# A decoder's state-space branch: its preparation cut into steps, and the second layer's moved beside the first attention

## The chip, the core and the metric

The kernel runs on one core of a Trainium2 chip. The core has five engines that each run their own instructions in order: TensorE (PE in the profile, with its weight loads as PEld), VectorE (DVE), ScalarE (ACT), GpSimd (POOL) and SyncE (SP, which issues most transfers). They wait for each other by semaphores. The metric is the time of one execution in microseconds (us), median of several runs.

## The reference

A decoder of four layers works on x, 4 batches of 256 tokens by 256 features, in float32. Each layer has an attention or a recurrence, a second branch that looks at a context, and a feed-forward part; each adds to x, and x is normalised after it. The change touches the first two layers:

```python
x = LN(x + attn0(x))            # multi-query attention, 16 heads of 128, rotary
x = LN(x + ssm0(context, z=x))  # selective state-space scan of the context
x = LN(x + thought(x))          # 4 iterations on the last token, gated into all tokens
x = LN(x + attn1(x))            # grouped-query attention (GQA), 16 heads of 16, 4 key heads
x = LN(x + ssm1(context, z=x))  # the same kind of scan with other weights
x = LN(x + moe(x))
```

The state-space branch takes only the context, until its last line, where x comes in as a gate:

```python
u     = silu(conv4(in_proj(context)) + conv_b)        # 256 channels e
dt, Bm, Cm = split(x_proj(u))                         # 8, 16 and 16 rows
delta = softplus(dt_proj(dt) + dt_proj_b)
A     = -exp(A_log)                                   # [256, 16]
state = state * exp(delta * A) + (delta * u) * Bm     # over the 256 tokens, 16 states n
y     = sum_n(state * Cm) + D * u
out   = y * silu(x)
```

So everything up to y can be worked out at any time before the gate, and only the gate and the sum into x stand in the layer's order.

## The kernel before

**Attention of layer 0, `run_mqa` (from L232).** 32 turns n, eight to a batch, each for four heads and one half of the batch's queries. A turn scales the shares of its softmax (reciprocal `sm`, L320), makes the scores of turn n + 1 and the queries of turn n + 4 (L281, from a PSUM pool `pm` of one bank), takes two scan steps (`K.scans.beside(2)`), turns the shares, projects turn n - 1 (`output`) and sums over the values (`sums`, copied out at L342). Turns 2 to 5 also make values and keys that are still missing.

**The scans, class `Scans` (L398 to 531).** The branch of a layer has a preparation and 64 scan steps (4 batches by 16 states). The preparation: four products of the convolution's taps with the input projection (four loads, four multiplications on GpSimd); the convolution as matrix products, in four groups of 128 channels by 512 tokens, each with an activation out of PSUM; Silu over the whole `u`; x_proj (copied at L474, stored to DRAM at L476 to be spread over the partitions later); dt_proj with a sum into `delta` (L115) and the absolute value into `du`; Exp, Ln and a maximum (L120) that make softplus; and `du = delta * u` on GpSimd. All of it is issued at once by `begin`. One scan step: a transfer of Bm and Cm rows to all partitions (`bc`, L513), two Exp on ScalarE (`dA`), a product on GpSimd (`s`, by the helper `ptt`, L123), the scan itself on VectorE (L520), a product with Cm (`s`, helper `tt`, L111), and, two steps later, a matrix product with the identity that adds it up in one PSUM bank (`ssmps`, helper `mm`, L132). `bc` and `s` have four buffers each, `dA` three. At the 16th state of a batch D * u is added (`u<-u,..,ssmps`, L120).

**The gate, `gate_pair` (L534).** It first takes scan steps until batch b is complete (`upto`), then Silu(x), a product on GpSimd, four transposes and the sum into x with its normalisation (`add_out`, `settle`, POOL's `rstd`). In the whole program the gates of layer 0 stand inside `run_mqa`, at turn 2 of the second batch after theirs began, the last behind turn 31; then the preparation of layer 1 is issued. Those of layer 1 stand inside the GQA.

**The thought, `run_thought` (L585).** First the gate (8 tiles: matrix products, additions of `gate_b`, one Sigmoid, L674 to 680), then the last token (`tok`, L686) and its normalisation, then four iterations of small operations that depend on each other (`tT` begins each, on [128, 8] tiles), and `lastmean`. GpSimd works out `gx` and `xb` from the gate and x, 24 scan steps are issued, and the result is gated into all tokens and normalised.

**GQA, `run_gqa` (L982).** A front part of eight tiles (products, rotary products `t0` to `t3`), each with a scan step, then 32 steps of the heads (`SmallHeads.run`), each with a scan step; a reciprocal `rec` (L915) ends each of eight units of four steps.

The order on each engine is made by a planner from the order of issue: an operation that is issued earlier has precedence, but a later one may go first where the planner expects it to be ready. So the place where the code takes a scan step is not exactly the place where the step stands on the engines.

## Time and profile before

| what | value |
|---|---|
| median of 3 runs | 2512.23 us (2508.54 to 2512.66) |
| profiled execution | 2505.99 us, span 2504.2 us |
| MQA, last reciprocal L320 | 380.9 us |
| layer 0's scans | 88.6 to 381.6 us |
| layer 1's scans | 467.4 to 771.4 us |
| thought, `tok` to `lastmean` | 431.8 to 519.6 us |
| GQA, first rotary product to end | 572.6 to about 800 us |

The page gives each engine's busy time and its share of the span. An engine that is busy for a large share isn't the bound everywhere: a stage can be bound by TensorE, and the next by a chain of small operations. A group's row gives line, engine, operation, output and inputs, how often, the duration of one (least, median, greatest in ns) and its first and last start. The program's later stages, from 800 us on, hold none of the edited code; they are two thirds of the span.

### The profile page before, as it was taken

Reading aid. Unit: us, or ns where it says so; the run is one execution under the profiler, and the core shown is the slowest. Engines: PE = TensorE matmul, PEld = TensorE weight load, DVE = VectorE, ACT = ScalarE, POOL = GpSimd, SP = SyncE. Lnnn points to the kernel's source line nnn. Section 1 sums busy time; section 2 is a strip of 40 time slices with the busy share of each in tenths; the row PEclk is TensorE's granted clock in tenths of the full one; section 3 lists DMA queues with packets and bytes.
Section 4 is the critical chain, followed back from the end, with each engine's and each line's share of the span. In section 5 each row is a group of like instructions: output and inputs, shape, how many; then the busy total and the mean of one; then the engine's idle time right before and its main releaser. Section 6 shows DMA issues by size and latency. Waiting matters only on the chain. (4 is left out here: it accounts for less than half of the span.)

```text
span 2504.2 us, 28859 instructions
## 1 busy us (share of the span) xinstructions
PE 2277.2 (91%) x10624; PEld 1526.3 (61%) x10624; DVE 1460.8 (58%) x2824; ACT 802.4 (32%) x1781; POOL 530.6 (21%) x617
## 2 busy tenths in 40 slices
PE   8798988648996999989999999999999989799997
PEld 5466654224443565545888888888776544476774
DVE  3798984588875412182356454444555667774556
ACT  3566663422442111153111111111122244343434
POOL 2544543663332222210001100011110002100001
PEclk9899999677987999999999999999988899999999
DMA  5221221122223254230123111211100002100000
GB/s 197 60 60 45 57 54 40 41 61 42 52 46 109 88 158 130 66 112 29 45 66 110 48 58 45 71 46 47 46 22 1 20 18 70 40 1 1 1 1 17
DMA packets 132836, 138.99 MB, mean 56 GB/s; under 512 B 13876, under 2 KB 120726, under 8 KB 130904
## 3 DMA queue, kind: packets, MB, share of 16 engines
q1 hardware_dynamic: 132696, 137.16, 19.1%
q8 instruction: 84, 1.38, 0.2%
q14 instruction: 56, 0.46, 0.1%
HBM read 134.27 MB, written 2.85 MB: 55 GB/s over the span
## 5 line engine op out<-in xcount | busy, mean ns | idle before, releaser
L132 PE MATMUL ps<-xw,xcT 128*128 128x256 f32 (+1 forms) x2304 | 519.0, 382 | 0.3 <-ACT YT L126 0.3
L132 PEld LDWEIGHTS ps<-xw,xcT 128*128 128x128 f32 x2304 | 430.7, 190 | 64.2 <-issue 1.9
L132 PE MATMUL sc<-kT,qT 32*128 32x256 f32 (+2 forms) x1024 | 240.7, 412 | 11.1 <-DVE qn L129 10.7
L520 DVE TENSOR_TENSOR_SCAN s<-dA,s 128x512 f32<-128x512 f32 x128 | 210.3, 1666 | 35.6 <-POOL s L123 35.4
L123 POOL TENSOR_TENSOR s<-du,bc 128x512 f32<-128x512 f32 x128 | 178.9, 1410 | 231.0 <-PE ssmps L132 191.1
L132 PEld LDWEIGHTS sc<-kT,qT 128*128 128x128 f32 (+1 forms) x1024 | 152.9, 206 | 92.3 <-issue 57.8
L132 PE MATMUL ssmps<-s,idz 128*128 128x512 f32 x256 | 147.1, 683 | 33.6 <-DVE s L111 33.5
L111 DVE TENSOR_TENSOR xp<-ps,xb 128x256 f32<-128x256 f32 x96 | 40.4, 421 | 227.0 <-PE ps L132 224.8
L126 ACT ACTIVATE dA<-delta,negA 128x255 f32<-128x255 f32 x256 | 117.7, 501 | 160.5 <-DVE s L520 160.3
L126 ACT ACTIVATE p<-sc,nm 128x256 f32<-128x256 f32 (+1 forms) x256 | 112.1, 445 | 109.5 <-DVE nm L129 103.7
L111 DVE TENSOR_TENSOR hT<-u,a 128x512 f32<-128x512 f32 x48 | 33.2, 691 | 186.1 <-PE u L132 186.1
L132 PE MATMUL o<-pT,vt 128*128 128x256 f32 (+1 forms) x352 | 121.1, 467 | 21.9 <-ACT pT L332 21.5
L123 POOL TENSOR_TENSOR xp<-xp,rn 128x128 f32<-128x128 f32 x96 | 35.2, 402 | 476.9 <-DVE rn L1406 476.9
L169 POOL TENSOR_SCALAR rstd<-mv 128x2 f32<-128x2 f32 x48 | 12.2, 255 | 551.3 <-DVE mv L161 541.4
L126 ACT ACTIVATE sq<-xp 128x1024 f32<-128x1024 f32 x24 | 25.4, 1057 | 314.3 <-DVE xp L111 314.2
L129 DVE TENSOR_REDUCE qn<-sc 128x2 f32<-128x480 f32 (+1 forms) x192 | 87.2, 506 | 43.6 <-PE sc L132 42.9
L129 DVE TENSOR_REDUCE nm<-sc 128x2 f32<-128x512 f32 (+1 forms) x128 | 77.2, 613 | 49.8 <-PE sc L132 49.2
L126 ACT ACTIVATE e<-sT 128x512 f32<-128x512 f32 x128 | 70.1, 591 | 108.3 <-PE sT L132 107.8
L1474 DVE TENSOR_TENSOR_SCAN dec<-xT,idz 128x256 f32<-128x256 f32 (+1 forms) x192 | 89.8, 537 | 25.0 <-DMA xT<-ad 25.0
L111 DVE TENSOR_TENSOR s<-s,bc 128x512 f32<-128x512 f32 x128 | 103.6, 829 | 1.1
L123 POOL TENSOR_TENSOR hT<-hT,sel 128x512 f32<-128x512 f32 x48 | 60.7, 1268 | 202.1 <-DVE hT L111 102.6
L132 PE MATMUL sT<-q,kT 32*128 32x256 f32 (+1 forms) x384 | 96.4, 502 | 1.7 <-ACT e L126 1.5
(503 smaller groups left out, 4067.1 us busy)
## 6 DMA issues: line engine op xcount, KB each, us to landing
bc<-bcd SPq DMA_DIRECT2D x128, 256.0 KB, 4.6
xw<-in_l2a_xw_dram SPq DMA_DIRECT2D x24, 768.0 KB, 4.9
xT<-ad SPq DMA_DIRECT2D x12, 1024.0 KB, 4.5
wj<-in_l1f_gate_dram SPq DMA_DIRECT2D x48, 128.0 KB, 2.6
wj<-in_l1f_up_dram SPq DMA_DIRECT2D x48, 128.0 KB, 3.1
wj<-in_l1f_down_dram SPq DMA_DIRECT2D x48, 128.0 KB, 3.5
sel<-cwd SPq DMA_DIRECT2D x32, 192.0 KB, 3.0
sel<-cwd SPq DMA_DIRECT2D x32, 128.0 KB, 3.5
```

The source lines that it names most:

```text
L111: self.nc.vector.tensor_tensor(out=out, in0=a, in1=b, op=op)
L123: self.nc.gpsimd.tensor_tensor(out=out, in0=a, in1=b, op=op)
L126: self.nc.scalar.activation(out, in_, func, **kw)
L129: self.nc.vector.tensor_reduce(out=out, in_=in_, axis=AX.X, op=op, **kw)
L132: self.nc.tensor.matmul(out, lhsT=lhsT, rhs=rhs, start=start, stop=stop)
L169: self.nc.gpsimd.tensor_scalar(out=out, in0=in_, scalar1=add, scalar2=None, op0=ADD)
L520: nc.vector.tensor_tensor_scan(out=s.rearrange("p c l -> p (c l)"), data0=dA.rearrange("p c l -> p (c l)"), data1=s.rearrange("p c l -> p ...
L1474: nc.vector.tensor_tensor_scan(out=dec[:, k, h, :], data0=ap[:, h, at(bb, k, j) : at(bb, k, 2)], data1=K.idz[:, 0 : (2 - j) * P], initial=0.0,
```

## The change

The preparation becomes a generator, `prepare(pre, bank)`, of 13 steps: taps; then for each half of the tokens (two batches) u, x_proj, dt_proj, Exp and Ln, and the combining of the two channel groups. Silu is applied straight out of PSUM, per 128x512 group; `u`, `delta` and `du` are tiles per half, with three buffers; the taps have tiles of their own, of one buffer; `du = delta * u` is on VectorE (`K.tt`) instead of GpSimd. The PSUM bank is given by the caller: in MQA it is that of the queries, `pm`. `start(pre)` begins the scan steps.

In MQA seven steps (taps, half 0 of layer 0) are issued before turn 0, with the scans' start; the other half follows in turns 2 to 7, one step in each; the 13 steps of layer 1 follow one in each turn from 19 on. The gates stand at turn 5 of the next batch instead of turn 2. Behind turn 31 the scans of layer 0 are completed, those of layer 1 started, gate 3 taken, and 8 scan steps of layer 1 issued. In the thought the gate's products, additions and Sigmoid are issued behind the first centring of the token instead of before `tok`, and 32 scan steps stand where 24 did. In GQA `upto` moves from `gate_pair` into its caller.

```diff
--- before.py
+++ after.py
@@ -355,9 +355,13 @@
                     K.add_out(2 * b + k, acc[b][:, k, :], not K.fused(0))

         N = 8 * B
+        bank = lambda: pm.tile([P, 512], F32, name="ps", tag="mm")
+        ahead = itertools.chain(K.scans.prepare("l0x", bank), K.scans.prepare("l1x", bank))
         keys(0)
         queries(0)
-        K.scans.begin("l0x")
+        for _ in range(7):
+            next(ahead)
+        K.scans.start("l0x")
         y = K.scans.y
         queries(1)
         values(0)
@@ -375,17 +379,24 @@
                 rest.pop(0)()
             if n == 6:
                 more()
+            if 1 < n < 8 or n > 18 and K.fused(0):
+                next(ahead, None)
             K.scans.beside(2)
             turn(n)
             if n:
                 output(n - 1)
             sums(n)
-            if n % 8 == 2 and n > 8 and K.fused(0):
-                gate_pair(K, wk, y, n // 8 - 1)
+            if K.fused(0):
+                if n % 8 == 5 and n > 8:
+                    gate_pair(K, wk, y, n // 8 - 1)
         output(N - 1)
         if K.fused(0):
+            K.scans.upto(B - 1)
+            for _ in ahead:
+                pass
+            K.scans.start("l1x")
             gate_pair(K, wk, y, B - 1)
-            K.scans.begin("l1x")
+            K.scans.beside(8)

@@ -410,6 +421,7 @@
         self.w = {}
         self.left = iter(())
         self.done = 0
+        self.ready = {}

     def load(self, pre):
         K = self.K
@@ -425,9 +437,17 @@

     def begin(self, pre):

-        self.left = self._steps(pre)
+        for _ in self.prepare(pre, self.bank):
+            pass
+        self.start(pre)
+
+    def start(self, pre):
+
+        self.left = self._steps(*self.ready[pre])
+        halves = self.ready[pre][1]
+
+        self.y = lambda b: halves[b // 2][0][:, :, b % 2 * L : b % 2 * L + L]
         self.done = 0
-        next(self.left)

     def beside(self, n):

@@ -439,55 +459,62 @@
         while self.done <= b:
             next(self.left, None)

-    def _steps(self, pre):
+    def prepare(self, pre, bank):
+
+
         K, nc, w, wk = self.K, self.K.nc, self.w[pre], self.wk
         cols = w["cols"]
-        N = B * L
-        u = self.one.tile([P, DC, N], F32, name="u", bufs=2)
-        delta = self.one.tile([P, DC, N], F32, name="delta")
-        du = self.one.tile([P, DC, N], F32, name="du")
+        negA = self.one.tile([P, DC, 16], F32, name="negA", bufs=2)
+        bc = self.dram.tile([2, 16, B * L], F32, name="bcd")
+        halves = []
+        self.ready[pre] = cols, halves, negA, bc


         taps = []
         for j in range(4):
-            t = wk.tile([P, D], F32, name="tap", tag="bc", padded_shape=[P, 2 * L])
+            t = self.one.tile([P, D], F32, name=f"tap{j}")
             nc.sync.dma_start(out=t, in_=K.A[f"{pre}_cw"][:, j * D : (j + 1) * D].to_broadcast([P, D]))
             K.ptt(t, t, w["in"], MUL)
             taps.append(t)
+        yield
+        K.act(negA, cols[:, :, 2:18], AF.Exp)
+        K.ts(negA, negA, -1.0, None, MUL)
         for h in range(2):
+
+            u, delta, du = (self.one.tile([P, DC, 2 * L], F32, name=n, bufs=3) for n in ("u", "delta", "du"))
+            halves.append((u, delta, du))
             for c in range(DC):
-                ps = self.bank()
+                ps = bank()
                 for j in range(4):
                     K.mm(ps, taps[j][:, c * P : (c + 1) * P], K.ctxp[:, 2 * h : 2 * h + 2, j : j + L], j == 0, j == 3)
-                K.act(u[:, c, 512 * h : 512 * h + 512], ps, AF.Identity, bias=cols[:, c, 0:1])
-        K.act(u, u, AF.Silu)
-        negA = self.one.tile([P, DC, 16], F32, name="negA")
-        K.act(negA, cols[:, :, 2:18], AF.Exp)
-        K.ts(negA, negA, -1.0, None, MUL)
-        bc = self.dram.tile([2, 16, N], F32, name="bcd")
-        for h in range(2):
-            s = slice(512 * h, 512 * h + 512)
+                K.act(u[:, c, :], ps, AF.Silu, bias=cols[:, c, 0:1])
+            yield
             xd = wk.tile([P, 512], F32, name="xd", tag="s")
-            ps = self.bank()
+            ps = bank()
             for c in range(DC):
-                K.mm(ps[0:40, :], w["xp"][:, c, :], u[:, c, s], c == 0, c == DC - 1)
+                K.mm(ps[0:40, :], w["xp"][:, c, :], u[:, c, :], c == 0, c == DC - 1)
             nc.scalar.copy(xd[0:40, :], ps[0:40, :])
             for k in range(2):
-                nc.sync.dma_start(out=bc[k, :, s], in_=xd[8 + 16 * k : 24 + 16 * k, :])
+                nc.sync.dma_start(out=bc[k, :, 2 * h * L : 2 * h * L + 2 * L], in_=xd[8 + 16 * k : 24 + 16 * k, :])
+            yield
             for c in range(DC):
-                ps = self.bank()
+                ps = bank()
                 K.mm(ps, w["dt"][:, c * P : (c + 1) * P], xd[0:8, :])

-                K.ts(delta[:, c, s], ps, cols[:, c, 1:2], None, ADD)
-                K.act(du[:, c, s], ps, AF.Abs, bias=cols[:, c, 1:2])
-        K.act(du, du, AF.Exp, scale=-1.0)
-        K.act(du, du, AF.Ln, bias=K.eps[1.0])
-        for c in range(DC):
-            K.stt(delta[:, c, :], delta[:, c, :], 0.0, du[:, c, :], MAX, ADD)
-            K.ptt(du[:, c, :], delta[:, c, :], u[:, c, :], MUL)
-
+                K.ts(delta[:, c, :], ps, cols[:, c, 1:2], None, ADD)
+                K.act(du[:, c, :], ps, AF.Abs, bias=cols[:, c, 1:2])
+            yield
+            K.act(du, du, AF.Exp, scale=-1.0)
+            K.act(du, du, AF.Ln, bias=K.eps[1.0])
+            yield
+            for c in range(DC):
+                K.stt(delta[:, c, :], delta[:, c, :], 0.0, du[:, c, :], MAX, ADD)
+                K.tt(du[:, c, :], delta[:, c, :], u[:, c, :], MUL)
+                yield
+
+    def _steps(self, cols, halves, negA, bc):
+        K, nc, wk = self.K, self.K.nc, self.wk
         turn = 0
-        self.y = u

         late = []
         bank = {}
@@ -499,18 +526,20 @@
             K.mm(y, K.ident, s.rearrange("p c l -> p (c l)"), n == 0, n == 15)
             if n == 15:
                 for c in range(DC):
-                    v = u[:, c, b * L : (b + 1) * L]
+                    lo = b % 2 * L
+                    v = halves[b // 2][0][:, c, lo : lo + L]
                     K.stt(v, v, cols[:, c, 18:19], y[:, c * L : (c + 1) * L], MUL, ADD)
                 self.done += 1

         for b in range(B):
-            lo = b * L
+            lo = b % 2 * L
             for n in range(16):
                 yield
+                _, delta, du = halves[b // 2]
                 if len(late) > 1:
                     add(*late.pop(0))
                 t = wk.tile([P, 2, L], F32, name="bc", tag="bc")
-                nc.sync.dma_start(out=t, in_=bc[:, n, lo : lo + L].unsqueeze(0).to_broadcast([P, 2, L]))
+                nc.sync.dma_start(out=t, in_=bc[:, n, b * L : b * L + L].unsqueeze(0).to_broadcast([P, 2, L]))
                 dA = self.dA[turn % 3]
                 turn += 1
                 for c in range(DC):
@@ -533,11 +562,10 @@

 def gate_pair(K, pool, y, b):

-    K.scans.upto(b)
     gate = pool.tile([P, DC, L], F32, name="gate")

     K.act(gate, K.x[:, 2 * b : 2 * b + 2, :], AF.Silu)
-    K.ptt(gate, gate, y[:, :, b * L : (b + 1) * L], MUL)
+    K.ptt(gate, gate, y(b), MUL)
     for t in range(2):
         ps = K.tp.tile([P, 512], F32, name="ps", tag="tp")
         for c in range(DC):
@@ -556,6 +584,7 @@
             wk = ctx.enter_context(K.tc.tile_pool(name="gate1", bufs=2))
             ctx.enter_context(K.turns())
             for b in range(B):
+                K.scans.upto(b)
                 gate_pair(K, wk, y, b)
         if pre == "l0x":
             K.scans.begin("l1x")
@@ -670,15 +699,6 @@
         cb = one.tile([P, DC], F32, name="cb")
         nc.vector.tensor_copy(cb, centred(d2b.unsqueeze(2), 1)[:, :, 0])

-
-        gate = one.tile([P, NT, D], F32, name="gate")
-        for i in range(NT):
-            ps = pm.tile([P, D], F32, name="ps", tag="mm")
-            for c in range(DC):
-                K.mm(ps, K.xT[:, c, i * P : (i + 1) * P], w["gate"][:, c, :], c == 0, c == DC - 1)
-            K.tt(gate[:, i, :], ps, row["gate_b"], ADD)
-        K.act(gate, gate, AF.Sigmoid)
-
         last = K.tp.tile([B, D], F32, name="last", tag="tp")
...
@@ -695,6 +715,15 @@
         th = one.tile([P, DC, B], F32, name="th")
         K.tt(th, ps, wide(w["cols"][:, 0, :], B), ADD)
         ct = centred(th, B)
+
+        gate = one.tile([P, NT, D], F32, name="gate")
+        for i in range(NT):
+            ps = pm.tile([P, D], F32, name="ps", tag="mm")
+            for c in range(DC):
+                K.mm(ps, K.xT[:, c, i * P : (i + 1) * P], w["gate"][:, c, :], c == 0, c == DC - 1)
+            K.tt(gate[:, i, :], ps, row["gate_b"], ADD)
+        K.act(gate, gate, AF.Sigmoid)
+

         K.stt(th, wide(d2b, B), 4.0, th, MUL, ADD)
         last = spare.tile([P, B], F32, name="last")
@@ -745,7 +774,7 @@
             K.ptt(gx[:, i, :], gate[:, i, :], row["bc_b"], MUL)
             K.ptt(gx[:, i, :], gx[:, i, :], K.x[:, i, :], ADD)
             K.ptt(xb[:, i, :], K.x[:, i, :], row["out_b"], ADD)
-        K.scans.beside(24)
+        K.scans.beside(32)

         def gated(b):

@@ -1030,7 +1059,12 @@
             K.scans.beside(1)
         early.close()
         if K.fused(3):
-            heads16.then = lambda b: gate_pair(K, wk, K.scans.y, b)
+
+            def then(b):
+                K.scans.upto(b)
+                gate_pair(K, wk, K.scans.y, b)
+
+            heads16.then = then
         heads16.run(ctx, lambda: K.scans.beside(1))
```

## The prediction

> **What bounds the kernel now.** I read the page's engine table first, then the 40 slices, then the table of windows cut at the stage marks of layers 0 and 1, then the rows of the scans and of the attention's reciprocals, and last the waits.
>
> ```profile
> span 2504.2 us, 28859 instructions
> PE 2277.2 (91%) x10624; PEld 1526.3 (61%) x10624; DVE 1460.8 (58%) x2824; ACT 802.4 (32%) x1781; POOL 530.6 (21%) x617
> PEclk9899999677987999999999999999988899999999
> ...
> 0.00:85.50 85.50, 73.68 (x259) 44.69 (x260) 33.45 (x54) 41.39 (x94) 20.12 (x34) 0.96 0.49 157
> 259.80:380.90 121.10, 107.64 (x468) 75.25 (x466) 104.78 (x141) 77.22 (x225) 58.87 (x44) 0.97 0.19 51
> 380.90:431.80 50.90, 44.73 (x150) 23.68 (x150) 19.93 (x40) 18.65 (x31) 14.43 (x29) 0.93 0.11 30
> 431.80:519.60 87.80, 55.53 (x254) 24.37 (x254) 55.74 (x61) 44.28 (x74) 52.93 (x43) 0.73 0.26 59
> 519.60:572.60 53.00, 23.73 (x55) 12.14 (x56) 44.89 (x92) 10.23 (x22) 29.93 (x33) 0.65 0.21 46
> 572.60:623.00 50.40, 45.23 (x183) 25.31 (x183) 42.24 (x85) 10.97 (x31) 20.18 (x38) 0.80 0.22 46
> 623.00:800.00 177.00, 156.52 (x971) 71.74 (x967) 129.98 (x193) 70.90 (x133) 53.38 (x53) 0.87 0.24 55
> ...
> L520 DVE TENSOR_TENSOR_SCAN s<-dA,s x128: 1185/1226/2298, 88.6 to 771.4; 128x512 f32<-128x512 f32 x128
> L320 DVE RECIPROCAL sm<-sm x32: 146/177/179, 25.0 to 380.9; 128x4 f32<-128x4 f32 x32
> L915 DVE RECIPROCAL rec<-o x8: 1745/1750/1758, 647.4 to 783.4; 128x256 f32<-128x256 f32 x8
> POOL s L123 <- PE ssmps L132: 91.1, 26, 12.4
> ```
>
> A window row gives its length, then the busy time of PE, PE's weight load, DVE, ACT and POOL, the granted clock, and the transfers' share and rate. The change ends where layer 1's grouped attention (GQA) ends, at 800 us. PE is full in the first attention (MQA: 107.6 of 121.1 us in its last 12 turns) and nearly so in GQA (156.5 of 177.0). Between them lies a chain: the four "thought" iterations, 431.8 to 519.6, with PE at 55.5 of 87.8 and a clock of 0.73, and the norm behind them, where DVE has 44.9 of 53.0. A scan step that moves out of a stage full on PE into this chain is cheap there only as long as POOL and DVE, which make it, don't hold the chain up. The last row says who paces the scans in GQA: POOL's product waits for PE's accumulation to release a buffer.
>
> Other rows that I use. The copies of L342 mark the ends of turns: 32.93, 85.53, 129.76, 358.01, 366.12, 374.26, 383.27, 391.02. Turns 4 to 27, with two scans each, take 10.7 us; those after the last scan 8.3. The first scan is at 88.6, the 64th at 381.6; layer 1's run from 467.4 to 771.4. The step `tok` of the thought is at 431.8, its iterations begin at 444.8, 466.1, 486.1 and 503.9.
>
> **The change, part by part.** "Scans ahead" is how many scan steps stand before a mark in VectorE's compiled order.
>
> 1. Start of MQA. Half 0 of layer 0's preparation is now issued ahead of the first scores. The chain of one half, from rows: tap loads to 31, two groups of four products (3.5 + 0.7 for the activation from PSUM), xd 1.9 + 0.6, two groups with delta and Abs 2.9 each, Exp and Ln with two table loads 4.6, the two combining operations 2.7, dA 1.3. First scan about 56 instead of 88.6. Turn 0's reciprocal then comes near 60 instead of 25, but the same PE work is done by turn 10 (138 us busy until its reciprocal at 166.7), and 19 scans stand ahead of it where 20 did. What remains is PE's waiting inside that chain, against the three turns from 32.9 to 85.5, which took 52.6 where 24.9 would do without a preparation (27.7 us its price). I take +3, ends -8 (the chain fills time that was idle) and +10. `du`'s multiply moves from POOL (2.8 us per 1024 columns) to DVE (about 1.2): it shortens the chain by 1.6 us at most.
>
> 2. Layer 1's preparation beside turns 19 to 31. It puts 24 products of 128x512 on PE (16 for the convolution, 4 + 4), 0.86 each: 20.6 us; some 21 on ACT, 8.3 on DVE, 2.8 on POOL. PE has 13.5 us free in the 121.1. Lower end 20.6 - 13.5 = +7; upper end 28, the 27.7 of layer 0. Of the 13 steps each is in a turn of its own, nearer to the lower end than layer 0's single block; against that, each group takes the one bank of the queries, which stays held until ACT or DVE has emptied it. I take +16. The queues that it passes: SP carries its four tap loads, which wait for the last convolution of layer 0 to release the tap tiles, and two stores per half; behind them stand the bc loads (4.6 us to landing, two steps of buffers in hand), so this costs nothing as long as layer 0's half 1 is through by turn 7. ScalarE gets 14 more table loads in the compiled order (63 to 77), 1.28 each. Its 77 busy us rise to about 98 of 121, so I hide them; without that cover they are 18 us.
>
> The Trainium skill ("ScalarE: Activation LUTs", section "Table sets: the hidden batching unit") speaks against this part: it wants calls of one set done together, while the change strews Silu, Exp and Ln between the attention's Exps. By that rule 14 loads of 1.28 us are +18 instead of none.
>
> 3. From the last reciprocal (380.9) to the end of the last iteration (519.6): 44 scans instead of 18. Up to `tok`: the preparation's products and the gate's 16 products with 8 additions leave, 9 scans enter (DVE 21 to 30 us of 50.9): -6. From `tok` to the first iteration: 13.0 us with no scan become 11 scans and the gate's products; at 2.4 a step that is 28: +15. First iteration: five scans instead of none, and 16 gx products of 0.72 on POOL (11.5 us in one block, waiting for the Sigmoid) hold the scans' products; DVE's chain stands behind those scans: 21.3 becomes about 24, +3. The others have six to seven scans, as the iteration of 486.1 had, which took 17.8: -2. Sum +10. The ends: -10, all steps at the 2.2 of the burst from 88.6 to 108.7 and overlapped with the chain; +25, all at 2.97 (17.8 / 6) with the POOL block on the path. Gate 3 waits for scan 64 as before; that `upto` now stands apart changes nothing.
>
> How close two SBUF users get on POOL and DVE decides this: a scan takes 1.2 us, but 2.27 at 88.57 and up to 2.30 where a product of POOL runs beside it. The Trainium skill ("SBUF — State Buffer", section "Who interferes with whom") has a DVE operation with two SBUF inputs and a GpSimd operation that reads SBUF exclude one another; by that a step is 1.27 + 1.23 + 0.68 = 3.18, and 44 make 140 us, longer than the whole stage's 138.7. The 2.2 of the burst say that the exclusion is not complete; a stage near 150 fits both.
>
> 4. From the last iteration to GQA's first rope product (53.0 us): six scans instead of nine, DVE-bound; three times 2.3: -7 (0 to -9).
>
> 5. GQA: 16 scans instead of 37. Ends: 0.86 each, PE's accumulation alone, -18; 1.91, all of DVE's work (1.23 + 0.68), -40. Nearest rows: a turn of MQA with two scans against one without, (10.7 - 8.3) / 2 = 1.2; GQA's units of one reciprocal (L915), 21.8 from 686.8 to 708.6 with four scans, 14.8 from 768.6 to 783.4 with none, 1.75. Both hold; I take the middle, 1.5: 21 x 1.5 = -31. What is late next there is PE, with 156.5 of 177 less 16.
>
> 6. Gates five turns into the next batch instead of two: POOL's product and four transposes meet other turns. Nothing: the scans they need (16 per batch, two a turn) have ended by then, and the last is where it was. Price if not: PE's waits for gate 3 in GQA, 6.8, are the nearest row; for three gates at most +5.
>
> Sum: +3 +16 +10 -7 -31 = -9 us. Against the profiled execution, 2505.99, that is 2497; the median of the runs shown lies 6.2 higher, so 2503.
>
> **Rivals.**
>
> A. More is hidden: preparation at its lower end (+7), the thought at 0, scans in GQA at their upper price (-40), the rest as above: 3 + 7 + 0 - 7 - 40 = -37, median 2475. For it: GQA's clock of 0.87 and 0.80 and DVE's 130 of 177. Against: POOL's 52.9 of 87.8 in the thought, before it gets 8 scans more.
>
> B, the other side: the small steps stall the turns. One mechanism, at L281's one PSUM bank: queries(n+4) and each preparation group take it in turn, a group is emptied by ACT or DVE behind the Exps, table loads and scans already queued there, and PE stands in order behind it. For it: in layer 0, one group to the next took 4.5 us (activations at 43.58, 48.06, 52.54) for 3.5 of PE. It decides from 14 us more than I gave (30 for 13 steps, 2.3 each). At 3 us for each step: 39 instead of 16, sum +14, median 2526. Against: queries are made four turns ahead.
>
> C. No change: the scans were never the bound in GQA, since PE is: 0.86 each, -18 instead of -31. Sum +4, median 2516. For it: the wait of 91.1 us of POOL for PE.
>
> **How the numbers follow.** The forecast has 0.36 (own range 2490 to 2507), A 0.18, C 0.14, B 0.32. A measurement of this kernel can tell about 0.2% (5 us) from no change. Faster: the forecast without a tenth of it, and A, 0.50; same, C and edges, 0.14; slower, B and the edge of C, 0.36. The range runs from A (2475) to beyond B, where the thought's upper end is added in part (2544).
>
> **What would show it.** Right: first scan near 56; the last reciprocal of L320 about 19 later than 380.9 and `tok` about 13 later than 431.8; the last iteration ended near 549, the first rope product near 595, the last reciprocal of L915 near 775. B shows as PE waits on the `ps` bank in turns 19 to 31 and a last reciprocal after 415; C as units of L915 that stay near 21 us with one or two scans each; A as a last reciprocal near 391. Wrong altogether: a bc load stuck on SP behind a tap load or a weight load, seen as POOL waiting for DMA in MQA beyond the 35.5 us of the whole span.

## The result

The changed kernel is slower: 2551.25 us median (2548.45 to 2559.34, 4 runs) against 2512.44 (2508.54 to 2522.53, 4 runs) for the kernel before in the same comparison, a ratio of 1.0153 with a 95% interval of 1.0115 to 1.0192. 2503 was forecast, and the range ended at 2544. The profiled execution took 2549.28 us with a span of 2547.5, 43.3 more than before.

One kernel's executions spread by more than one per cent here: the kernel before ran from 2493.8 to 2529.0 over all comparisons below. Its time goes with the granted TensorE clock: two of its executions on one chip had a mean of 0.946 at a span of 2492.0 us and of 0.932 at 2517.9. So single profiles are compared by stages, and kernels by ratios of several runs.

### The profile page after: what moved, and what is told of

It reads as the page before. It is cut to its first block, busy times and chain, and to the rows that moved or that the text cites. A ratio compares the mean times of both kernels' runs of the same rounds, so it can differ in the third digit from the quotient of the medians.

```text
span 2547.5 us, 28882 instructions
## 1 busy us (share of the span) xinstructions
PE 2296.7 (90%) x10624; PEld 1537.3 (60%) x10624; DVE 1463.8 (57%) x2836; ACT 817.8 (32%) x1797; POOL 517.7 (20%) x613
## 5 line engine op out<-in xcount | busy, mean ns | idle before, releaser
L549 DVE TENSOR_TENSOR_SCAN s<-dA,s 128x512 f32<-128x512 f32 x128 | 207.6, 1641 | 50.9 <-POOL s L123 47.5
L132 PE MATMUL ssmps<-s,idz 128*128 128x512 f32 x256 | 154.8, 716 | 59.4 <-DVE s L111 37.9
L132 PE MATMUL o<-pT,vt 128*128 128x256 f32 (+1 forms) x352 | 119.4, 462 | 10.4 <-ACT pT L332 9.9
L132 PEld LDWEIGHTS ssmps<-s,idz 128*128 128x128 f32 x256 | 50.8, 220 | 104.5 <-issue 51.3
L126 ACT ACT_TABLE_LOAD x77 | 98.8, 1283 | 21.4 <-DVE x L117 12.8
L132 PE MATMUL sT<-q,kT 32*128 32x256 f32 (+1 forms) x384 | 102.2, 521 | 3.6 <-ACT e L126 3.4
```

What stands on the lines that cost most here:

```text
L126: self.nc.scalar.activation(out, in_, func, **kw)
L132: self.nc.tensor.matmul(out, lhsT=lhsT, rhs=rhs, start=start, stop=stop)
L549: nc.vector.tensor_tensor_scan(out=s.rearrange("p c l -> p (c l)"), data0=dA.rearrange("p c l -> p (c l)"), data1=s.rearrange("p c l -> p ...
```

## The profile after

The page first: TensorE's share and work are much as before, and its clock row has more dips in the first third.

```profile
span 2547.5 us, 28882 instructions
PE 2296.7 (90%) x10624; PEld 1537.3 (60%) x10624; DVE 1463.8 (57%) x2836; ACT 817.8 (32%) x1797; POOL 517.7 (20%) x613
PEclk8999999676888799999999999999998889999999
```

Then the same stages as in the prediction, cut at the changed kernel's own marks: start, turns 19 to 31, from there to `tok`, to the first iteration, that iteration, the other three, the norm, and the front part of GQA. (Length, busy time of PE, PEld, DVE, ACT and POOL, clock, transfers.)

```profile
0.00:109.10 109.10, 77.27 (x249) 46.95 (x249) 46.58 (x65) 47.05 (x107) 28.83 (x41) 0.86 0.45 139
...
274.40:425.00 150.60, 134.65 (x516) 85.22 (x515) 109.28 (x151) 98.74 (x248) 55.56 (x43) 0.95 0.19 43
425.00:469.90 44.90, 28.45 (x87) 13.82 (x88) 31.81 (x43) 18.95 (x36) 26.81 (x30) 0.80 0.31 78
469.90:507.40 37.50, 28.42 (x86) 18.22 (x86) 26.73 (x41) 15.72 (x32) 14.81 (x12) 0.70 0.30 73
507.40:534.80 27.40, 13.72 (x59) 7.29 (x60) 16.91 (x17) 9.82 (x19) 24.18 (x24) 0.73 0.19 43
534.80:589.70 54.90, 38.63 (x176) 14.50 (x174) 50.46 (x47) 27.11 (x53) 29.45 (x21) 0.84 0.41 89
589.70:631.10 41.40, 19.36 (x49) 10.95 (x50) 35.04 (x82) 7.03 (x16) 25.65 (x37) 0.61 0.15 38
```

Set against the marks of before, the 43.3 us divide like this (profiled executions; "turn 10" is the 11th reciprocal of L320):

| stretch | before | after | difference | forecast |
|---|---|---|---|---|
| start to turn 10 | 166.7 | 177.8 | +11.1 | +3 |
| turn 10 to 19 | 93.0 | 96.6 | +3.6 | 0 |
| turn 19 to 31 | 121.1 | 150.6 | +29.5 | +16 |
| to `tok` | 50.9 | 44.9 | -6.0 | -6 |
| to the first iteration | 13.0 | 37.5 | +24.5 | +15 |
| first iteration | 21.3 | 27.4 | +6.1 | +3 |
| other three, to `lastmean` | 53.4 | 54.8 | +1.4 | -2 |
| norm, to the first rope product | 53.0 | 41.5 | -11.5 | -7 |
| GQA, to its last reciprocal | 210.9 | 190.5 | -20.4 | -31 |
| rest of the program, unedited | 1720.8 | 1725.9 | +5.1 | 0 |

The signs of all of the prediction's terms came out but one small one (the other three iterations); the sizes didn't, and each large miss but that of the norm went the same way. The rest of the program is no effect of the change: over the kernels below it lasted from 1714.8 to 1737.3.

In turns 19 to 31 TensorE is busy 134.65 of 150.6 us: 27 more than the 107.64 before, and it waits about as long as before (16.0 against 13.5). That is a full engine with more work, not a chain of waits. Of its waits there, those for the softmax (`sm`, `pT`) stayed at 7.4 us where they were 7.6, and a new one of 4.1 is for the preparation's own `du` (the changed kernel, then the kernel before):

```profile
PE ssmps L132 <- DVE sm L320: 4.1, 1, 4.1
PE ps L132 <- ACT du L126: 4.1, 2, 2.1
PE o L132 <- ACT pT L332: 3.3, 2, 2.8
```

```profile
PE o L132 <- ACT pT L332: 7.6, 3, 4.7
```

In the start it is the other way round. The rows of TensorE there, with what ended each wait, are those of one half's preparation with nothing beside it:

```profile
33.83 3.70 PE L132 MATMUL ps<-ctxp,tap 128*128 128x512 f32 x8 [0.78 <-ACT u L126]
38.31 1.91 PE L132 MATMUL ps<-u,w_l0x_xp 128*40 128x512 f32 x4 [0.78 <-ACT u L126]
40.89 1.12 PE L132 MATMUL ps<-xd,w_l0x_dt 8*128 8x512 f32 x2 [0.67 <-ACT xd L496]
43.57 1.12 PE L132 MATMUL ps<-xd,w_l0x_dt 8*128 8x512 f32 x2 [1.56 <-ACT du L126]
46.26 3.78 PE L132 MATMUL ps<-xT,w_q 128*128 128x256 f32 x8 [1.56 <-ACT du L126]
52.32 2.05 PE L132 MATMUL ps<-w_l0a_wkv,xT 128*128 128x128 f32 x8 [2.28 <-DVE ropet L111]
...
63.76 3.75 PE L132 MATMUL ps<-xT,w_q 128*128 128x256 f32 x8 [5.48 <-DVE ropet L111]
```

The first scan came at 57, as forecast (56). But from 22 to 70 us TensorE was busy 30.5 of 48 us at a clock of 0.72, where the kernel before has 47.7 at 0.96 (windows of after, then of before):

```profile
22.00:70.00 48.00, 30.54 (x77) 17.61 (x77) 20.03 (x26) 20.49 (x41) 12.63 (x10) 0.72 0.46 142
```

```profile
22.00:70.00 48.00, 47.73 (x170) 27.82 (x169) 16.71 (x30) 25.77 (x65) 9.43 (x10) 0.96 0.43 134
```

Of the 17.2 us of work that TensorE is behind by then, it makes up 10.4 in the next 40, in which the kernel before waits for its first scans (after, then before):

```profile
70.00:110.00 40.00, 38.37 (x152) 24.16 (x151) 20.37 (x29) 24.35 (x60) 12.45 (x11) 1.00 0.14 34
```

```profile
70.00:110.00 40.00, 27.99 (x89) 16.04 (x90) 28.60 (x29) 22.70 (x48) 22.58 (x12) 0.84 0.16 35
```

The sign that the prediction named for a transfer stuck on SP did not come: up to 430 us GpSimd waited 3.0 us for `bc`, where it had waited 8.6 before.

In the thought's first iteration GpSimd's block of gx stands between the scans' products, and VectorE waits 9.34 us for the one behind it, with the iteration's own chain queued after that scan (GpSimd, then VectorE):

```profile
507.21 3.06 POOL L123 TENSOR_TENSOR s<-du,bc 128x512 f32<-128x512 f32 x2
510.23 2.33 POOL L123 TENSOR_TENSOR gx<-gate,r_l0f_rows 128x256 f32<-128x256 f32 x2
512.51 2.77 POOL L123 TENSOR_TENSOR gx<-gx,x 128x256 f32<-128x256 f32 x2
...
522.52 1.40 POOL L123 TENSOR_TENSOR gx<-gx,x 128x256 f32<-128x256 f32 x2
523.88 6.30 POOL L123 TENSOR_TENSOR s<-du,bc 128x512 f32<-128x512 f32 x4
```

```profile
525.17 2.27 DVE L549 TENSOR_TENSOR_SCAN s<-dA,s 128x512 f32<-128x512 f32 x1 [9.34 <-POOL s L123]
```

## The experiments

The theory after the result (W): the preparation costs its TensorE work wherever TensorE is full, so turns 19 to 31 are a bad place; the chain ahead of the scores costs TensorE's waits; and scans in the thought stand ahead of a chain in VectorE's order. The rival from the prediction (B): the shared bank, table loads and in-order waits stall the turns.

### Undoing one part of the change at a time

**Layer 1's preparation behind gate 3 again.**

```diff
-            if 1 < n < 8 or n > 18 and K.fused(0):
+            if 1 < n < 8:
                 next(ahead, None)
...
             K.scans.upto(B - 1)
+            gate_pair(K, wk, y, B - 1)
             for _ in ahead:
                 pass
             K.scans.start("l1x")
-            gate_pair(K, wk, y, B - 1)
             K.scans.beside(8)
```

> The changed kernel with layer 1's preparation taken out of turns 19 to 31 and issued in one go behind gate 3, as the kernel before has it; all else stays. Theory W (the preparation costs its TensorE work where TensorE is full, and less where a chain leaves TensorE idle): the last reciprocal of L320, 425.0 in the changed kernel, comes at 395 to 399; half of the gain is kept behind turn 31, the first iteration begins 15 to 25 us earlier than 507.4, and the median falls by 15 to 25 from 2551 to 2526-2536. Rival P (the same TensorE work only changes its place): the last reciprocal moves as above, but the first iteration begins within 5 us of 507 and the median stays within 5 of 2551. Rival S (the turns are slow for another reason, gates or softmax): the last reciprocal stays after 415.

Measured: last reciprocal at 390.7, first iteration at 483.5, 24 before the changed kernel; but the median 2544.55, ratio 1.0139 (1.0087 to 1.0192), no clear gain. Turns 19 to 31 took 116.9 us, so in those turns the preparation costs 33.7. Counting each TensorE instruction from the end of the one before, its products are 22.4 of that (14.2 for the convolution, 4.4 and 3.8 for the other two), other products that ran slower 5.9, and waits 5.5. `lastmean` was 20 us earlier, yet the first `rec` of GQA was where it had been (693.7 against 694.0). GQA's front is where the gain went. It took 82.4 us instead of 62.9, with ten scans in it instead of six and at a lower clock (0.73 against 0.86), half of the full one for three stretches with TensorE busy all the time:

```profile
640.00:650.00 10.00, 10.00 (x23) 5.33 (x24) 6.30 (x12) 0.38 (x2) 1.60 (x2) 0.50 0.18 42
650.00:660.00 10.00, 8.64 (x42) 4.94 (x43) 6.87 (x13) 3.33 (x8) 2.21 (x5) 1.00 0.15 37
660.00:670.00 10.00, 10.00 (x32) 5.55 (x32) 4.05 (x7) 1.19 (x2) 1.14 (x1) 0.51 0.12 27
670.00:680.00 10.00, 10.00 (x28) 4.35 (x26) 6.73 (x9) 3.74 (x8) 1.39 (x2) 0.50 0.15 30
```

So W holds for the turns; what the gain is worth at the end wasn't settled by this kernel, and the shares of the four scans and of the clock weren't told apart.

**Layer 0's preparation whole, at the old place.**

```diff
-        ahead = itertools.chain(K.scans.prepare("l0x", bank), K.scans.prepare("l1x", bank))
+        ahead = K.scans.prepare("l1x", bank)
...
-        for _ in range(7):
-            next(ahead)
-        K.scans.start("l0x")
+        K.scans.begin("l0x")
...
-            if 1 < n < 8 or n > 18 and K.fused(0):
+            if n > 18 and K.fused(0):
```

> The changed kernel with layer 0's preparation issued whole, at the place and from the bank of the kernel before, instead of half 0 ahead of the first scores and half 1 in turns 2 to 7; layer 1's stays in turns 19 to 31. Theory: the start's 11 us (turn 10's reciprocal at 177.8 against 166.7) are TensorE's waits in the bare chain of half 0; that reciprocal comes at 166 to 170, everything behind it 8 to 11 earlier, median 2540 to 2543. Rival: the start's loss is that of the small steps (halved activations, table loads), which this kernel keeps: turn 10 stays at 174 or later, median 2547 or more.

Turn 10's reciprocal at 156.9: 20.9 earlier, twice what was expected, and 9.8 earlier than in the kernel before. The median fell to 2531.67, ratio 1.0096 (1.0067 to 1.0125). The places (half 0 ahead of the scores, half 1 in turns 2 to 7) and their bank therefore cost about 21 us together. The pieces themselves bring 5 to 10, which the prediction had at next to nothing: in the five kernels that have all of them, with this layer's preparation whole, turn 10 comes at 156.9 to 161.3. That most of the loss is the chain ahead of the scores is seen in TensorE, which has no hole in the same window as above:

```profile
22.00:70.00 48.00, 46.27 (x170) 26.11 (x169) 21.72 (x34) 32.91 (x73) 15.73 (x16) 1.00 0.50 147
```

**The thought's gate ahead of `tok` again.** (The eight lines of products, additions and Sigmoid move back.)

> The changed kernel with the thought's gate ahead of tok again, as before. If the late gate is what makes the stretch from tok to the first iteration long (37.5 us against 13.0), that stretch falls to 18 to 24 and the one before it grows by 8 to 12: the first iteration begins 5 to 10 earlier than 507.4. If the scans that stand there make it long, it begins within 4 of 507.4 or later.

From `tok` to the first iteration 21.4 us instead of 37.5, and that iteration began at 492.1, 15.3 earlier, with no loss in the stretch before (44.9 again). But six scans went with it: five stand in that stretch, where the changed kernel has 11. The other iterations took 62.8 instead of 54.8 (21 scans instead of 19), GQA's front 79.1 instead of 62.9 (ten scans instead of six, at a clock of 0.74), and the last `rec` came at 826.1, no earlier than 821.6. From the last reciprocal to `lastmean` the kernel took 153.0 us instead of 164.7, so the late gate and four scans together cost 11.7 in the thought, and undoing the gate's place alone doesn't bring the end forward.

**Gates at turn 2 again.** (`n % 8 == 5` becomes `n % 8 == 2`.)

> The changed kernel with the gates at turn 2 of the next batch, as before; everything else stays. If the turn in which a preparation group and gate 1 meet (20.4 us, from 306.9 to 327.3) is long because of that meeting, turns 19 to 31 fall from 150.6 to 140-146. If the gates' place is worth something by itself, as between the other kernels, they take 152 to 158. If neither, 148 to 152.

Turns 19 to 31 took 149.3 us, 1.3 less than in the changed kernel, in one execution of each: neutral, and the long turn is not made by the gate.

### Work or waiting in the turns

**One convolution tap for layer 1.** (`for j in range(4)` becomes one product for `l1x`.)

> The changed kernel with one convolution tap instead of four for layer 1 alone: 12 of its 16 products are left out, so its result for that layer differs; banks, activations, table loads and steps stay as they are. If TensorE's work is the price in turns 19 to 31 (12 products at 0.86 are 10.3 us), the last reciprocal comes 9 to 11 before 425.0. If the price is waiting (the shared bank, table loads, the order behind ScalarE; rival B of the prediction), it moves by less than 4.

The last reciprocal came at 419.5, 5.5 earlier, but this execution's turn 19 was 1.6 later; turns 19 to 31 took 143.5 us against 150.6, and against 152.9 in two other kernels with the same turns (layer 0's preparation whole above, and gx on VectorE below). So 7 to 9 of the 10.3 us of products left out came off. Work, then, for most of it. That spread of 2.3 us is also what single executions of the next two kernels can't resolve.

**The transposes' two banks instead of the queries' one.**

```diff
-        ahead = itertools.chain(K.scans.prepare("l0x", bank), K.scans.prepare("l1x", bank))
+        ahead = itertools.chain(K.scans.prepare("l0x", bank), K.scans.prepare("l1x", lambda: K.tp.tile([P, 512], F32, name="ps", tag="tp")))
```

> The changed kernel with layer 1's preparation in the two banks of the transposes instead of the one bank of the queries. If sharing the queries' bank costs (rival B of the prediction), turns 19 to 31 take 140 to 146 us from reciprocal to reciprocal, where the changed kernel took 150.6; if TensorE's work is the price, they take 148 to 153.

150.9 us. No cost of sharing the queries' bank is seen; rival B falls with its mechanism, though the price that it gave for the turns (39) is nearer to the measured one than the forecast's. What the rows show of its kind is the 4.1 us for `du`.

**No table loads for layer 1.** (Silu and Ln of its preparation become Identity.)

> The changed kernel with Silu and Ln of layer 1's preparation replaced by Identity, so that its table loads go and its result for that layer differs. If the ten table loads in turns 19 to 31 (12.8 us of ScalarE, eight more than without the preparation) stand in the way of the softmax, those turns take 140 to 146 instead of 150.6; if ScalarE's idle time hides them, 148 to 152.

152.9 us. The groups of ScalarE's table loads in those turns, in the changed kernel and then without Silu and Ln:

```profile
L126 ACT ACT_TABLE_LOAD x10 | 12.8, 1283 | 3.1 <-PE ps L132 1.5 <-DVE x L117 1.4
```

```profile
L126 ACT ACT_TABLE_LOAD x2 | 2.6, 1283 | 1.5 <-DVE x L117 1.4
```

Ten loads became two, and the turns didn't get shorter: ScalarE, busy 98.7 of 150.6 us, hides them. The Trainium skill ("ScalarE: Activation LUTs", section "Table sets: the hidden batching unit") wants calls batched by set. The price that the prediction worked out from that rule, 18 us for 14 loads, did not show in these turns, where ScalarE had idle time.

**gx on VectorE.** (`K.ptt(gx..` becomes `K.tt(gx..`, twice.)

> The changed kernel with the 16 gx products of the thought on VectorE (about 0.42 each, 6.7 us) instead of GpSimd. If GpSimd's block of gx holds the scans' products, and so the chain behind them in VectorE's order, the iteration that begins at 507.4 shrinks from 27.4 to 18-22 us, some of it given back where VectorE does the products; median 2543 to 2548. If the chain of scans itself sets that iteration, it stays within 2 us, and the median rises by up to 5 for VectorE's new work.

First iteration 18.4 us instead of 27.4, with four scans in it instead of five: GpSimd's block was what held it, for all but what that one scan costs. Median 2542.25, ratio 1.0139 (1.0088 to 1.0190), not told apart from the changed kernel's: its GQA front took 72.8 instead of 62.9, with 2 scans more and a clock of 0.77 against 0.86.

### One part of the change alone

**The new preparation at the old places.** `prepare` as changed, but both layers by `begin` in one go, gates at turn 2, the gate of the thought early, 24 steps.

> The kernel before with the new preparation alone: by halves, Silu straight out of PSUM, taps in tiles of their own, du's multiplication on VectorE; but issued whole and at the old places (layer 0's behind the first queries, layer 1's behind gate 3), with the gates at turn 2, the thought's gate ahead of tok and 24 steps, as before. Theory W: the pieces are good and their places are bad: turn 10's reciprocal near 157 as in the kernel with layer 0's whole (166.7 before), all else as before; median 5 to 12 below that of before. Rival: the gain at the start is used up by the first scans' fewer or by half clocks later, median within 5 of before.

2501.0 us against 2509.49, ratio 0.9961 (0.9940 to 0.9983): faster than before. Turn 10 at 159.4.

**The same with the gates at turn 5.**

> The new preparation alone (whole, at the old places), with the gates of batches 0 to 2 at turn 5 of the next batch, as the change has them, instead of turn 2. In the stages of the kernels so far, turns 19 to 31 took 123.2 us with gates at turn 2 and 118.6 with gates at turn 5. If the later gates are worth that by themselves, the last reciprocal comes at 368 to 374 instead of 380.0 and the median is 4 to 10 below the 2501 of the new preparation alone, 0.990 to 0.994 of before. If they are neutral (the prediction's part 6), the last reciprocal stays after 377 and the median within 3 of 2501.

2493.98 against 2509.07, ratio 0.9927 (0.9892 to 0.9961), the lowest ratio of the kernels that have an interval. The last reciprocal came at 374.6, between the two expectations, with turns 19 to 31 at 118.6; `lastmean` was only 1.8 earlier than in the kernel with gates at turn 2 (521.3 against 523.1). Whether the later gates are a gain isn't told apart: the two intervals overlap, and in the changed kernel they were neutral.

**That with gx on VectorE.**

> The same with the gx products on VectorE. In the changed kernel that made the first iteration 9 us shorter (27.4 to 18.4). Here 5 scans fewer stand beside that iteration (24.4 us): if GpSimd's block holds it too, it takes 17 to 20, and the median is 3 to 8 below that of the kernel with gates at turn 5; if not, within 3 of it.

2504.39 us, ratio 0.9964 (0.9933 to 0.9994). The first iteration, with four scans in both kernels (one fewer than in the changed kernel, not five), fell from 24.7 to 19.8, but 3.0 us went to the stretch before, 2.2 to the iterations behind and 5.3 to the norm, where VectorE is full and eight scans stand instead of six: no gain.

**That kernel with gates at turn 5, and the thought's part of the change added.** Gate of the thought behind the token's chain, 32 steps, 8 steps behind gate 3.

> The changed kernel with both preparations whole and at the old places; what stays of the change is the gate of the thought behind the token's chain, 32 scan steps in the thought, gates at turn 5. If the scans from turn 31 on are worth their place (20 fewer in GQA), it is 5 to 15 faster than the new preparation alone; if the thought's chain gives back what GQA gains, it is within 5 of it; if the thought's part loses by itself, 5 to 20 slower, with the first iteration beginning after 465 where the kernel before has 444.8.

2517.94 us, ratio 1.0026 (1.0001 to 1.0051): the last expectation, the thought's part loses by itself. From the last reciprocal to `lastmean` 179.6 us instead of 146.7 (24.7 + 53.4 of them in the iterations, 27.5 + 59.4 here), with 40 scans instead of 26: +32.9, or 2.35 a scan if all of it is put down to them, the late gate included. From there to the last `rec` 244.4 instead of 250.9: -6.5 for 14 scans fewer, 0.46 a scan. Even that isn't sure: the kernel with layer 1's preparation behind gate 3 has its scans in the same stages as this one and took 250.9 there, no less than with 40. The stretch from `tok` to the first iteration holds the preparation and 13 scans, and took 63.6 us where it was 14.1 (this kernel, then the one without the thought's part):

```profile
399.00:462.60 63.60, 48.48 (x136) 24.12 (x136) 44.27 (x57) 38.67 (x61) 21.43 (x17) 0.79 0.33 68
```

```profile
429.10:443.20 14.10, 9.64 (x34) 5.61 (x34) 7.96 (x14) 7.63 (x10) 11.88 (x15) 0.74 0.08 17
```

**What of the pieces makes the start faster.** In the kernel with gates at turn 5, `du`'s multiplication back on GpSimd, then Identity out of PSUM with one Silu per half behind it.

> The kernel with the new preparation whole, at the old places, gates at turn 5, but du's multiplication on GpSimd as before. If that multiplication (2.8 us per 1024 columns on GpSimd) is what makes the start late in the kernel before, turn 10's reciprocal comes at 164 to 168 instead of 157 to 161, and the first scan at 75 or later instead of 67 to 69. If not, they stay within 2 of 161 and 69.

> The same kernel (du on VectorE) with Identity out of PSUM and one Silu over each half behind it, as before per layer, instead of Silu straight out of PSUM. If the extra Silu and its wait for both groups are what makes the start late, turn 10's reciprocal comes at 164 to 168; if the gain is that the first half's scans needn't wait for the second half, it stays at 157 to 162 with this and with du on GpSimd.

Turn 10 at 156.0 and 157.3, first scans at 68 and 69: neither piece by itself makes the gain. What is left is the taps' own tiles, and that the scans of half 0 no longer wait for half 1's preparation. For the second speaks GpSimd: in the kernel before, its first products for the scans stand straight behind `du` of all the tokens, without waiting for a transfer, and in the kernel with gates at turn 5 they come 17.5 us earlier (before, then gates at turn 5):

```profile
81.60 5.60 POOL L123 TENSOR_TENSOR du<-delta,u 128x1024 f32<-128x1024 f32 x2 [2.95 <-DVE delta L120]
87.28 6.77 POOL L123 TENSOR_TENSOR s<-du,bc 128x512 f32<-128x512 f32 x4
```

```profile
69.77 4.64 POOL L123 TENSOR_TENSOR s<-du,bc 128x512 f32<-128x512 f32 x3
```

The waits of TensorE from 22 to 160 us fit that, before and then in the kernel with gates at turn 5; the scans' late start no longer stands in its way:

```profile
PE ssmps L132 <- DVE s L111: 11.3, 4, 7.9
```

```profile
PE ssmps L132 <- DVE s L111: 2.6, 1, 2.6
```

That it is this was reached by exclusion and from these rows; no run joined the halves again, and none gave the taps their old tiles.

### The ladder

Each row adds one part to the row above; ratios are to the kernel before in the same comparison.

| kernel | ratio | interval | step |
|---|---|---|---|
| preparation by halves, issued whole at the old places | 0.9961 | 0.9940 to 0.9983 | -0.4% |
| + gates at turn 5 | 0.9927 | 0.9892 to 0.9961 | -0.3%, not clear |
| + thought: late gate, scans from turn 31 on | 1.0026 | 1.0001 to 1.0051 | +1.0% |
| + layer 1's preparation in turns 19 to 31 | 1.0096 | 1.0067 to 1.0125 | +0.7% |
| + half 0 of layer 0 ahead of the scores, half 1 in turns 2 to 7: the change | 1.0153 | 1.0115 to 1.0192 | +0.6% |

The places lose what the pieces gain, and more. The last step is the least clear of the three losses, since its two intervals overlap a little; its stage, the start, shows it by itself (20.9 us). The order of the rows matters for one of them: taking layer 1's preparation out of the full change brought only 0.1% (1.0139 against 1.0153), so its net price lies between that and 0.7%.

## Why the prediction was wrong

It forecast -9 us and got +39, and it erred in the sizes of five terms of its sum.

- **Part 1, start (+3; measured +11.1, and +3.6 more by turn 19).** Its step "the same PE work is done by turn 10" was right (133 us of matrix products, 137 before) and its conclusion wrong: TensorE lost 17 us of busy time from 22 to 70 at 0.72 of its clock and made up only 10 of them from 70 to 110, when it was full. Two effects hid each other: the places cost about 21, the pieces bring 5 to 10. The prediction saw neither at its size; its -8 for the lower end was nearly what the pieces do alone, for another reason.
- **Part 2, turns 19 to 31 (+16; measured +29.5).** The failing step is "nearer to the lower end than layer 0's single block": it let 20.6 us of products fill 13.5 us of idle time. They didn't; waiting time even grew, from 13.5 to 16.0. The waits for the softmax stayed (7.6, then 7.4), and the preparation brought one of its own (4.1). The nearest row, 27.7 us for layer 0's preparation, was near the right price (29.5, or 33.7 against the kernel with the preparation behind gate 3), and the forecast set it as the upper end.
- **Rival B** named the right loss in the right place, and its sign, a last reciprocal after 415, came (425.0), but with the wrong mechanism: neither the bank (150.9) nor the table loads (152.9) made it, and TensorE's waits on the preparation's groups are 4.1 us.
- **Part 3, the thought (+10; measured +26.0).** The step "at 2.4 a step that is 28" gave +15 for the stretch ahead of the first iteration, where +24.5 came. What failed is that this counts the 11 scans alone and lets them hide the gate's products and additions: 37.5 us came. With the gate early, and five scans, that stretch took 21.4; the shares of the gate and of the other six scans in these 16 us aren't told apart. The price of 2.4 itself is about what came later (2.35, gate included), though its lower bound was misread: eight scans start between 88.6 and 108.7 us, so that burst ran at 2.9 a step and not at 2.2. The gx block was named, at +3 net; without it the iteration was 9 shorter.
- **Part 4, the norm (-7; measured -11.5).** Right in sign and in the six scans. But the two kernels with the new preparation at the old places have 41.2 and 41.5 there too, also with six scans, so it belongs to the order of the scans and not to the 44 ahead; that the term came out is in part luck.
- **Part 5, GQA (-31; measured -20.4).** The step that failed is the price of 1.5 a scan, from stages with and without scans; 21 scans fewer gave 0.97 each in this execution and 0.46 to 1.04 in the five other kernels with the same scans, whose two stages took 189.1 to 201.2 us together; 14 fewer gave 0.46 or nothing between other kernels. That is about rival C's 0.86, TensorE's accumulation alone: C was right here, though not on the whole. The higher row, units of 21.8 against 14.8 us, took the last unit as one without a scan, but it has one, at 771.4, and it is shorter than others for other reasons too: the last four units took 74.8 us with 13 scans in the kernel before and 66.1 with none in the changed one, 0.67 a scan.
- **Part 6, the gates, and the 14 table loads** were costed at nothing, and nothing clear of the spread was seen of either.

So the change as a whole moved scans from a place where they cost about 1 us or less to one where they cost 2.35 with the late gate. The prediction had both prices in its bounds (0.86; 2.2 to 2.97); it took a favourable middle, 1.5, for the first, and for the second a fair one, but with nothing for the gate.

## What to carry to other kernels

An engine that is busy nine tenths of a stage doesn't offer its last tenth: price work moved there at its full duration on that engine, and more (here 33.7 us for 22.4 of products). Work moved beside a chain of short dependent steps isn't free because engines are idle there: ahead of that chain in their queues it was paid for here; that it would be free behind the chain was not tried. And cut a large preparation so that its first half can be used early, but leave it where other work covers its waits.

## What was not expected of the hardware

GQA's front part changes length with the granted clock even where the work is the same. Six kernels have the same six scans in it (112 ahead of it, 118 at its end), and but for a few instructions at its edges the same order on each engine. It lasted 62.4 us at a mean clock of 0.86, 62.7 at 0.86, 62.9 at 0.86, 68.5 at 0.77, 70.3 at 0.76 and 73.8 at 0.72 (the third and the last, the changed kernel and the one with the transposes' banks):

```profile
631.10:694.00 62.90, 58.90 (x310) 31.60 (x310) 47.24 (x98) 15.59 (x41) 18.38 (x38) 0.86 0.14 31
```

```profile
628.10:701.90 73.80, 70.46 (x314) 36.55 (x312) 48.08 (x99) 15.74 (x41) 18.36 (x38) 0.72 0.13 26
```

These 11 us are as large as the effects that were to be measured. The scans in it count too, or go with the clock: with eight of them it lasted 69.6 to 75.4 us in five kernels, with ten 78.4 to 82.4 in three. In the three experiments whose gains were gone by the first `rec`, two or four scans more and a lower clock came together.

The half clock comes here while TensorE works. In the changed kernel it holds from 663 to 680 us; the products of 32 rows (`sc`, `sT`) of the heads run in it, with no recorded wait between 665 and 680:

```profile
665.02 2.80 PE L132 MATMUL sc<-kT,qT 32*128 32x256 f32 x9 [0.74 <-DVE qn L129]
667.04 1.21 PE L132 MATMUL sT<-q,kT 32*128 32x512 f32 x1
...
670.74 2.08 PE L132 MATMUL ssmps<-s,idz 128*128 128x512 f32 x2
...
679.21 1.22 PE L132 MATMUL sc<-kT,qT 32*128 32x256 f32 x4
680.22 1.10 PE L132 MATMUL sT<-q,kT 32*128 32x512 f32 x4
681.16 0.59 PE L132 MATMUL sc<-kT,qT 32*128 32x256 f32 x4
681.68 1.12 PE L132 MATMUL ssmps<-s,idz 128*128 128x512 f32 x2
```

The accumulation's two passes take 2.08 us at 670.74 and 1.12 at 681.68. The Trainium skill ("TensorE: Matmul & The Clock Gate", section "Part 1: The HAM clock gate (the "warmup" mystery)") has the clock come back to full after about 3.4 us of sustained work. Here 15 us of work without a recorded wait passed first, so the measurement differs from that page; what made the clock drop and stay was not tried.
